# A planned one-core graph/convolution/GRU kernel on Trainium2: residual loaded a batch ahead, tanh and mix chained by expected times, third weight added behind its load, VectorE given background work further ahead

## The chip, the cores and the metric

The kernel runs on one core of one Trainium2 chip. The metric is the device time of one execution in microseconds. Before the change it is 2330.36 us, the median of three runs (2320.62 to 2338.33).

## What is computed

The input `x` is 32 batches of 512 nodes with 256 channels; `adj` is a 0/1 matrix of 512 x 512 for each batch. All is float32. Cut to what matters (`d` = 256):

```python
h  = relu(layernorm(x))
xc = transpose(h)                                          # channels first
c  = bn2(conv1d_17taps(relu(bn1(conv1d_1tap(xc)))))
x_conv = transpose(relu(c + xc))
s   = h @ w_se.T + b_se                                    # 3 numbers per node
A   = exp(-dist(s, s)) * adj
msg = relu(h @ w_msg.T + b_msg)
x_nmp = einsum('bnm,bmd->bnd', A, msg)
gi = concat([x_conv, x_nmp]) @ w_ih.T + b_ih
gh = h @ w_hh.T + b_hh
r, z = sigmoid(gi_r + gh_r), sigmoid(gi_z + gh_z)
n  = tanh(gi_n + r * gh_n)
out = x + (1 - z) * n + z * h
```

## The kernel before, in words

**Tiles and stages.** Channels lie on the 128 partitions (two halves, `ND` = 2), nodes along the free dimension; P is 128. Each batch goes through six streams, each a Python generator that issues instructions and then says when it can go on:

- `begins` and `rows` (`begin`, `norm_t`, `conv1`; L320, L770, L785): the normalised input is turned by TensorE, stored to DRAM (`hd`), and the 1-tap convolution writes into `h1`. The layer norm's statistics are background work of VectorE (`norm`, L273).
- `graphs` (`graph`, L794): `messages` (tiles `msg`, `aug`), `factors` and `factors_t` (`augl`, `augr` turned into `left`, `right`), `kernel_exp` (four matmuls and Exp into `at`), `masked` (four times a mask times `at`), `gather` (`at` times `msg`, copied into `right` and stored to DRAM as `nd`).
- `conv` (`convolution`, L610): the 17 taps by a two-level product scheme: batches in groups of four, eight groups of 25 products. Product m needs the operand `X2[m]` (tiles `x`, VectorE), the weight `WS[m]` (tile `w`) and, from group 1 on, `XD[m]` (tile `xd`, VectorE). Results go through PSUM tiles `ps_c` and `ps_b` and are summed by VectorE into `n`, `z` and `y` (`summed`, L485). In group 0 the weights are made by VectorE and ScalarE (`weights_first`, L425) and stored; in group 1 two thirds of each weight are loaded and the last third is added by VectorE (`third_weight`, L473); later groups load all three.
- `gates` (`gates`, L824): `evacuate` (L555) copies `y` into `xconv`; then the products with `whh` and `wih` in PSUM tiles `ps_acc`, sigmoid, tanh (`mix`, L889) and three VectorE operations into `o_sb` (`mix_last`, L858).
- `finish` (L753): TensorE turns `o_sb`, VectorE adds the original input (tile `res`, loaded by `load_res`, L763), SyncE stores it.

**What sets the order.** Nothing reorders at run time: each engine and each engine's DMA queue goes through its list in order, and waits on semaphores. The lists are made by a planner in the kernel itself (L936 to L1049). It keeps a clock `now` of TensorE's planned work and, for VectorE and ScalarE, the planned time `free` at which each is done. In each step it picks, among streams whose awaited time has come, the one with the smallest `clock` and lets it issue up to its next `yield`. If none is able, `now` moves on by 0.25. After each step `fill` (L964) issues what was put off with `later`, tries one `evacuate`, and gives VectorE background work (operands, sums, statistics, weights) while `dve.free < now + 0.5`. A `yield act.free + 0.2` thus says: go on 0.2 us after ScalarE's planned end. The planner knows of no DMA queue, of no PSUM bank that must be emptied before its next use, and of no activation table load.

**Loads around the change.** Nearly all loads and the output stores are issued on SyncE's queue. `load_res(b)` is called by `mix_last` of batch b, ahead of the loads of the next batch's sums (`load_sums`, tiles `xnb`), and the finish of batch b comes at least 6 planned us later. The two `res` tiles of a batch fill the pool's two buffers. `w` has three buffers; its loads wait for the product that last read the buffer. PSUM: three banks for `ps_g` (shared by turning, messages, exp, gather and 1-tap convolution), two for `ps_acc`, two for `ps_c`, one for `ps_b`.

Of the kernel before, what the change touches and what calls it, by code (L numbers as in the profile page):

```python
# [44 lines left out]
def kernel(  # L45
# [50 lines left out]


    now = 10.0

    def elements(t):  # L100
        n = 1
# [40 lines left out]

    def later(t, f):
        LATER.append((t, f))

    def settle():
        while LATER:
# [125 lines left out]
    def norm(b):  # L273

        xs = XS[b]
        st = front.tile([P, NT, 6], F32, name="st")
        mv = front.tile([P, NT, 2], F32, name="mv")
        for c in range(NT):
            dve.bn_stats(st[:, c, :], xs[:, c, :])
            dve.bn_aggr(mv[:, c, :], st[:, c, :])  # L280
            if c % 2:
                yield 0.0
        rstd = front.tile([P, NT], F32, name="rstd")
        rsqrt(rstd, mv[:, :, 1])
        yield dve.free + 1.5
        shift = front.tile([P, NT], F32, name="shift")
        dve.scalar_tensor_tensor(
            shift, mv[:, :, 0], -1.0, rstd, op0=ALU.mult, op1=ALU.mult
        )
        yield dve.free + 0.2  # L290
        for c in range(NT):
            act.activation(
                xs[:, c, :], xs[:, c, :], AF.Identity, bias=shift[:, c : c + 1],
                scale=rstd[:, c : c + 1],
            )
            if c % 2:
                yield act.free + 0.2

    def norm_some(b):

# [124 lines left out]
    def weights_first():  # L425


        outer = [
            taps_of(
                lambda k, i=i: wraw[:, i, :, :, k, :],  # L430
                lambda i=i: prep.tile([P, 2, 3, D], F32, name=f"g{i}", bufs=1),
                True,
            )
            for i in range(ND)
        ]
        for j1 in ORDER:
# [12 lines left out]
            for j2 in ORDER:  # L449
                gg = []  # L450
                for i in range(ND):
                    gg.append(next(inner[i]))
                    yield 0.0
                yield dve.free + 0.1
                w = new_w()
                for i in range(ND):
                    act.activation(
                        w[:, :2, i, :], gg[i], AF.Copy, scale=GSCALE[j1] * GSCALE[j2]
                    )
                nc.scalar.dma_start(WD[len(WS)][:, :2], w[:, :2])  # L460
                WS.append(w)
                W_AT.append(act.free + 0.2)
                yield 0.0

    def weights_again(m):
# [19 lines left out]
    def summed(g):  # L485
# [29 lines left out]
        for j1 in ORDER:  # L515
# [30 lines left out]
                for f in range(3):  # L546
                    add(y[:, :, f], y[:, :, f], z, ALU.subtract if (f, j1) == (1, 2) else ALU.add)
        SUMS.append(lambda: EVAC.extend(
            (y, b, o) for b in range(g * G, (g + 1) * G) for o in range(ND)
        ))  # L550
        yield

# [1 line left out]

    def evacuate():  # L555

        y, b, o = EVAC[0]
        if b >= G and b - G not in gated or act.free > now + 0.3:
            return False
        EVAC.pop(0)  # L560
        act.behind(dve)
        if o == 0:
            XC[b] = late.tile([P, ND, Q * U], F32, name="xconv", bufs=4)
        c = o * NU + b % G * U
        act.activation(
            XC[b][:, o, :].rearrange("p (u h k) -> p k h u", h=2, k=9),
            y.rearrange("p e f (h n) -> p (e f) h n", h=2)[:, :, :, c : c + U],
            AF.Identity, bias=bn2_sh[:, o : o + 1], scale=bn2_sc[:, o : o + 1],
        )
        if o == ND - 1:  # L570
            evacuated[b] = act.free + 0.2
        return True

    AHEAD = 3
# [11 lines left out]
    def operand_some():  # L586

        nonlocal freed
        if len(X2) >= min(at_product + 1 + AHEAD, 25 * NG) or len(X2) >= 25 * made:
            return False  # L590
        if len(X2) == 25 * (made - 1) and now < made_at:
            return False
        got = next(xs)
        if got is not None:
            X2.append(got)
            X_AT.append(dve.free + 0.2)
            if len(X2) % 25 == 21:
                freed = len(X2) // 25
        return True
# [10 lines left out]
    def convolution():  # L610
# [18 lines left out]
        for g in range(NG):  # L629
# [3 lines left out]
            for n in range(25):  # L633
# [5 lines left out]
                if m == 24:  # L639
                    late_pools()  # L640
                yield lambda: len(X2) > m and len(WS) > m
                if 25 <= m + 1 < 50:
                    third_weight(m + 1)
                for k in (m, m + 1):
                    if 25 <= k < len(X2) and k not in XD:
                        XD[k] = ends(X2[k])
                        X_AT[k] = dve.free + 0.2
# [40 lines left out]
    def messages(b, msg, c):  # L688
# [3 lines left out]
        dve.tensor_tensor(gr.aug[:, c, :3], ps[:, D:], bmsg[:, D:], op=ALU.add)  # L692
        if c % 2:
            m = msg[:, c - 1 : c + 1, :]
            later(dve.free + 0.1, lambda: act.activation(m, m, AF.Relu))

    def factors():
        aug, augl = gr.aug, gr.augl
# [48 lines left out]
    def gather(b, msg, at, d):  # L747
        ps = bank()
        matmul_sum(ps, [(msg[:, c, d * P : (d + 1) * P], at[:, c, :]) for c in range(NT)])
        act.activation(gr.right, ps, AF.Copy)  # L750
        nc.scalar.dma_start(ND_[b, d], gr.right)

    def finish(b, o_sb, c):  # L753
        ps = bank()
# [6 lines left out]
        nc.sync.dma_start(out[b].rearrange("(c p) d -> p c d", p=P)[:, c : c + 2, :], y)  # L761

    def load_res(b):  # L763
        for c in range(0, NT, 2):
            XR[b, c] = late.tile([P, 2, D], F32, name="res", bufs=2)
            nc.sync.dma_start(XR[b, c], x[b].rearrange("(c p) d -> p c d", p=P)[:, c : c + 2, :])

# [17 lines left out]
    def rows(b):  # L785
        nonlocal made, made_at
        for o in range(ND):
            conv1(b, o)
            if o == ND - 1 and b % G == G - 1:
                made, made_at = b // G + 1, act.free + 0.2  # L790
            yield now
        HT.pop(b, None)

    def graph(b):  # L794
# [18 lines left out]
        yield act.free + 0.2  # L813
        for n in range(NT):
            masked(b, at, n)
            if n < NT - 1:
                yield dve.free - 0.4
        settle()
        yield dve.free + 0.2
        for d in range(ND):  # L820
            gather(b, msg, at, d)
            yield now
# [1 line left out]
    def gates(b):  # L824
# [26 lines left out]
        def residual():  # L851
            xconv = XC.pop(b)[:, :, :N]
            dve.tensor_tensor(xconv, xconv, hT, op=ALU.add)
            yield dve.free + 0.1
            act.activation(xconv, xconv, AF.Relu)
            x_in.extend([xconv[:, i, :] for i in range(ND)] + [XN[b, d] for d in range(ND)])

        def mix_last(r, z, o):  # L858
            t = o_sb[:, o, :]
# [2 lines left out]
            dve.tensor_tensor(t, r, t, op=ALU.add)  # L862
            if o == ND - 1:
                unfinished[b] = o_sb
                load_res(b)
                load_sums(b + 1, 0)
                load_sums(b + 1, 1)

        for o in range(ND):
            r = z = None  # L870
# [17 lines left out]

            def mix():  # L889
                dve.tensor_tensor(r, ps_n, r, op=ALU.add)  # L890
                later(dve.free + 0.1, lambda r=r, o=o: act.activation(
                    r, r, AF.Tanh,
                    bias=vec[:, _COL["b_ih"] + 2 * ND + o : _COL["b_ih"] + 2 * ND + o + 1],
                ))
                later(dve.free + 1.0, lambda r=r, z=z, o=o: mix_last(r, z, o))

            ps_r = acc.tile([P, N], F32, name="ps_acc")
            if o == 0:
# [4 lines left out]
                yield act.free + 0.2  # L903
# [15 lines left out]
    def all_finishes():  # L919
        for b in range(B):  # L920
            yield lambda: b in unfinished
            yield max(dve.free, now + 6.0)
            for c in range(0, NT, 2):
                finish(b, unfinished[b], c)
                yield now


    bn1_sc, bn1_sh = bn_affine("bn1")
# [13 lines left out]
        return True  # L942

    def norm_ahead(early=0.45):
        for b in list(NORMS):
# [37 lines left out]
    def all_rows():  # L983
        nonlocal rows_wait
        for b in range(B):
            if b < G:
                yield from begin(b)
                yield act.free + 0.2
# [7 lines left out]

    def all_gates():
        yield lambda: late is not None
        for b in range(B):
            yield from gates(b)  # L1000

# [97 lines left out]
```

## Time and profile before

| what | us |
|---|---|
| median of three runs | 2330.36 |
| the profiled execution's own time | 2333.51 |
| its span, first to last instruction | 2331.6 |
| TensorE busy | 2186.6 (94%) |
| VectorE busy | 1453.7 (62%) |
| ScalarE busy | 783.0 (34%) |
| mean granted TensorE clock | 0.975 |

In the rows of the profile PE is TensorE, DVE VectorE, ACT ScalarE, SP SyncE; "SPq" is SyncE's DMA queue issuing a transfer. A row of a group or of the timeline names the line, the engine, the operation, the tile written and the tiles read, the shape, and the count; in square brackets, or behind the second bar, stands the idle time of the engine just before and what ended it. A float32 matmul of the program stands as two in the trace. Nearly every row has L126, L131 or L117, since helpers issue for all streams; so one goes by the tiles' names. In a row of the windows view stand, for each engine, its busy time and number of instructions, then the granted TensorE clock and the share of the DMA engines in use.

### The profile page before, as it was taken

The page shows a single profiled execution, that of the slowest core. Times are in us where ns is not written, and L with a number is a line of the kernel's source. Part 1 is how long each engine was busy: PE and PEld are TensorE (multiplying, and loading weights), DVE is VectorE, ACT ScalarE, POOL GpSimd, SP SyncE. Part 2 cuts the span into 40 slices and gives each one's busy share as a digit, 9 for nine tenths or more (in the row PEclk, how much of TensorE's full clock was granted, in tenths as well). Part 3 has the DMA queues.
Part 4 walks back from the last instruction along what each step waited for, and adds up shares of the span by engine and source line. Part 5 has one row for each costly group of instructions (what it writes and reads, how often), then busy time and mean ns, then how long its engine had stood idle before and what let it go on. Part 6 is the DMA issues. An engine that isn't in the chain of part 4 may idle for free.

```text
span 2331.6 us, 26175 instructions
## 1 busy us (share of the span) xinstructions
PE 2186.6 (94%) x9640; PEld 1359.6 (58%) x9640; DVE 1453.7 (62%) x2700; ACT 783.0 (34%) x1318; POOL 60.6 (3%) x73
## 2 busy tenths in 40 slices
PE   5888989999989999999989998999999999999998
PEld 3765655566556656566556565655656656566443
DVE  6566667767666666766556665666766846576422
ACT  5342432134322333234412334223432334222411
POOL 1000000000000000000000000000000000000000
PEclk9998989999999999999999999999999999999999
DMA  6343454455544545554355534556545535444121
GB/s 248 125 148 117 178 181 149 136 199 149 167 140 140 185 127 163 151 160 152 127 162 157 176 114 131 166 158 176 163 134 155 158 132 158 153 136 136 50 73 45
DMA packets 328270, 342.40 MB, mean 147 GB/s; under 512 B 214160, under 2 KB 263696, under 8 KB 327504
## 3 DMA queue, kind: packets, MB, share of 16 engines
q1 hardware_dynamic: 308720, 287.52, 40.6%
q10 hardware_dynamic: 17424, 46.67, 5.2%
q0 software_dynamic: 2000, 6.56, 0.7%
q8 instruction: 76, 1.25, 0.2%
q14 instruction: 50, 0.41, 0.1%
HBM read 270.68 MB, written 69.99 MB: 146 GB/s over the span
## 4 chain that ended last, share of the span: by engine, by line
PE 83%; DVE 6%; ACT 5%; DMA 4%; issue 1%; SPq 0%; ACTq 0%; DVEq 0%
PE ps_acc L126 40%; PE ps_g L126 17%; PE ps_c L126 16%; PE ps_b L126 6%; PE ps_g L131 3%; DMA nd<-right 1%; PE ps_b L724 1%; DMA res<-in_x_dram 1%; DVE o_sb L117 1%; ACT at L117 1%; ACT r L117 1%; DMA w<-wd 1%; DMA xnb<-nd 1%; DVE x L117 1%; ACT L117 1%
## 5 line engine op out<-in xcount | busy, mean ns | idle before, releaser
L126 PE MATMUL ps_acc<-hTb,whh 128*128 128x512 f32 x768 | 366.3, 607 | 13.3 <-ACT r L117 13.3
L126 PE MATMUL ps_c<-xd,w 128*128 128x116 f32 x2800 | 349.6, 279 | 21.1 <-DVE xd L117 12.2
L126 PE MATMUL ps_acc<-xconv,wih 128*128 128x512 f32 x768 | 363.9, 596 | 4.6 <-ACT xconv L117 4.6
L126 PE MATMUL ps_acc<-xnb,wih 128*128 128x512 f32 x768 | 362.7, 594 | 2.8 <-DMA xnb<-nd 2.6
L126 PEld LDWEIGHTS ps_c<-xd,w 128*128 128x128 f32 x2800 | 334.2, 195 | 25.3 <-DVE xd L117 13.1
L126 PE MATMUL ps_g<-at,msg 128*128 128x512 f32 x512 | 233.5, 604 | 11.8 <-DVE at L117 10.2
L126 PEld LDWEIGHTS ps_acc<-hTb,whh 128*128 128x128 f32 x768 | 142.9, 194 | 169.8 <-issue 141.9
L126 PEld LDWEIGHTS ps_acc<-xnb,wih 128*128 128x128 f32 x768 | 141.5, 189 | 165.1 <-issue 158.2
L126 PEld LDWEIGHTS ps_acc<-xconv,wih 128*128 128x128 f32 x768 | 141.8, 191 | 160.3 <-issue 149.7
L126 PEld LDWEIGHTS ps_b<-x,w 128*128 128x128 f32 x1400 | 182.8, 193 | 77.1 <-issue 58.0
L117 DVE TENSOR_TENSOR r<-ps_acc,r 128x512 f32<-128x512 f32 x64 | 44.2, 691 | 267.0 <-PE ps_acc L126 267.0
L126 PE MATMUL ps_b<-x,w 128*128 128x116 f32 x1400 | 185.6, 276 | 7.2 <-ACT at L117 7.0
L117 ACT ACTIVATE mid<-ps_b 128x232 f32<-128x232 f32 x175 | 63.6, 363 | 339.2 <-PE ps_b L126 322.3
L126 PEld LDWEIGHTS ps_g<-at,msg 128*128 128x128 f32 x512 | 96.9, 194 | 126.5 <-issue 109.5
L117 DVE SCALAR_TENSOR_TENSOR r<-ps_acc,vec,r 128x512 f32<-128x512 f32 x64 | 48.0, 751 | 184.1 <-PE ps_acc L126 149.5
L126 PE MATMUL ps_g<-wmsg,hTg 128*128 128x259 f32 x512 | 131.9, 395 | 23.2 <-DVE aug L117 13.2
L117 DVE SCALAR_TENSOR_TENSOR x<-x,x 128x480 f32<-128x480 f32 (+1 forms) x184 | 143.8, 782 | 2.0
L117 ACT ACTIVATE right<-ps_g 128x512 f32<-128x512 f32 x96 | 57.3, 597 | 257.7 <-PE ps_g L126 227.5
L117 ACT ACTIVATE z<-ps_acc,brz 128x512 f32<-128x512 f32 x64 | 43.9, 686 | 276.0 <-PE ps_acc L126 275.9
L117 DVE TENSOR_TENSOR x<-x 128x240 f32<-128x240 f32 (+1 forms) x320 | 135.6, 462 | 0.3
L126 PEld LDWEIGHTS ps_g<-wmsg,hTg 128*128 128x128 f32 x512 | 97.3, 196 | 61.6 <-issue 35.3
L126 PE MATMUL ps_g<-hT,w 128*128 128x512 f32 x256 | 123.9, 630 | 3.9 <-ACT hT L117 2.7
(101 smaller groups left out, 2463.5 us busy)
## 6 DMA issues: line engine op xcount, KB each, us to landing
w<-wd SPq DMA_DIRECT2D x150, 768.0 KB, 4.6
m_sb<-in_adj_dram SPq DMA_DIRECT2D x384, 64.0 KB, 2.6
hd<-hT ACTq DMA_DIRECT2D x32, 512.0 KB, 5.0
hTg<-hd SPq DMA_DIRECT2D x32, 512.0 KB, 3.6
nd<-right ACTq DMA_DIRECT2D x64, 256.0 KB, 2.1
hTb<-hd SPq DMA_DIRECT2D x32, 512.0 KB, 5.2
xnb<-nd SPq DMA_DIRECT2D x64, 256.0 KB, 3.1
res<-in_x_dram SPq DMA_DIRECT2D x64, 256.0 KB, 4.0
```

The lines of the kernel that those rows point to most:

```text
L117: getattr(self.engine, name)(*tiles, **more)
L126: nc.tensor.matmul(ps, lhsT, rhs, **more)
L131: nc.tensor.transpose(ps, a, ident)
L724: nc.tensor.matmul(pss[c], gr.left[k, :], gr.right[k, :], start=True, stop=True, tile_position=(32 * c, 0),)
```

## The change

1. `load_res(b + 1)` is called behind the finish of batch b (and `load_res(0)` when the gates start). The finish of b no longer waits for `now + 6`, but for `dve.free + 0.6`. `load_sums` of the next batch is issued by the last `mix`, not by `mix_last`.
2. `later` keeps its list sorted by time. `mix` puts off only the tanh; the tanh (`mix_next`) then puts off `mix_last` to 0.3 behind its planned end.
3. `third_weight` is added a product ahead only if the weight's load is planned to have landed, else at its own product; the product then waits for the planned end of the addition.
4. `fill` gives VectorE background work while `dve.free < now + 1.5`, where it was 0.5.
5. Most waits for VectorE or ScalarE have one margin, `LAG` = 0.6, where they had 0.1 to 0.3. `evacuate` waits until the planned end of the sums has passed. Of the statistics only the first two batches in line are tried. The second gather of a batch uses a part of `at` in place of `right`. The gates' clock starts at 1.25 instead of 1.2.

The diff, cut to its core:

```diff
 def later(t, f):
     LATER.append((t, f))
+    LATER.sort(key=lambda e: e[0])
...
+thirds = set()
 def third_weight(m):
+    if m in thirds:
+        return
+    thirds.add(m)
     w = WS[m]
     dve.tensor_tensor(w[:, 2], w[:, 0], w[:, 1], op=ALU.add)
     nc.gpsimd.dma_start(WD[m % 25][:, 2], w[:, 2])
+    W_AT[m] = dve.free + LAG
...
 def evacuate():
-    y, b, o = EVAC[0]
-    if b >= G and b - G not in gated or act.free > now + 0.3:
+    t, y, b, o = EVAC[0]
+    if now < t or b >= G and b - G not in gated or act.free > now + 0.3:
         return False
     EVAC.pop(0)
-    act.behind(dve)
...
     # convolution, before product m
-    if 25 <= m + 1 < 50:
+    if 25 <= m + 1 < 50 and W_AT[m + 1] <= now:
         third_weight(m + 1)
...
     yield max(X_AT[m], W_AT[m])
+    if 25 <= m < 50:
+        third_weight(m)
+        yield W_AT[m]
...
 def gather(b, msg, at, d):
...
-    act.activation(gr.right, ps, AF.Copy)
-    nc.scalar.dma_start(ND_[b, d], gr.right)
+    sums = gr.right if d == 0 else at[:, 0, :]
+    act.activation(sums, ps, AF.Copy)
+    nc.scalar.dma_start(ND_[b, d], sums)
...
     # graph
     factors()
     load_graph(b + 1)
-    yield dve.free + 0.2
+    yield dve.free + LAG
     factors_t()
...
-    yield act.free + 0.3
+    yield act.free + LAG
     kernel_exp(at)
-    yield act.free + 0.2
+    yield act.free + 0.3
...
+def mix_next(r, z, o):
+    act.activation(r, r, AF.Tanh, bias=...)
+    later(act.free + 0.3, lambda: mix_last(r, z, o))
 def mix_last(r, z, o):
...
     if o == ND - 1:
         unfinished[b] = o_sb
-        load_res(b)
-        load_sums(b + 1, 0)
-        load_sums(b + 1, 1)
 def mix():
     dve.tensor_tensor(r, ps_n, r, op=ALU.add)
-    later(dve.free + 0.1, lambda r=r, o=o: act.activation(r, r, AF.Tanh, bias=...))
-    later(dve.free + 1.0, lambda r=r, z=z, o=o: mix_last(r, z, o))
+    later(dve.free + 0.3, lambda r=r, z=z, o=o: mix_next(r, z, o))
+    if o == ND - 1:
+        load_sums(b + 1, 0)
+        load_sums(b + 1, 1)
...
 def all_finishes():
     for b in range(B):
         yield lambda: b in unfinished
-        yield max(dve.free, now + 6.0)
+        yield dve.free + LAG
         for c in range(0, NT, 2):
             finish(b, unfinished[b], c)
             yield now
+        load_res(b + 1)
...
 def fill():
...
-    while dve.free < now + 0.5 and background():
+    while dve.free < now + 1.5 and background():
...
-    "gates": (all_gates(), 125.0, 1.2),
+    "gates": (all_gates(), 125.0, 1.25),
```

Since these numbers feed the planner, the lists of all engines change. Three places follow, as the lists stand before and with the change.

SyncE's queue around the end of the gates of batch 9 of 32 (`res` is the residual, `xnb` the sums of the next batch, `w` a convolution weight, `hT` and `hTb` stored inputs). Before:

```order
L264 DMA m_sb<-in_adj_dram 32x16x32 x12
L766 DMA res<-in_x_dram 128x2x256 x2
L185 DMA xnb<-nd_0_132 128x512
L185 DMA xnb<-nd_1_133 128x512
L469 DMA w<-wd_230 128x1536
L761 DMA out_dram<-res 128x2x256 x2
L469 DMA w<-wd_231 128x1536
```

With the change:

```order
L187 DMA xnb<-nd_0_132 128x512
L187 DMA xnb<-nd_1_133 128x512
L171 DMA hT<-hd_98 128x1024
L471 DMA w<-wd_232 128x1536
L772 DMA out_dram<-res 128x2x256 x2
L777 DMA res<-in_x_dram 128x2x256 x2
L171 DMA hT<-hd_99 128x1024
```

The load of `res` stood two loads and a weight ahead of the store that ends the same batch; now it stands right behind that store and is for the next batch.

TensorE in group 0 of the convolution, at the third graph before and the second with the change (`wmsg` products are the messages, `augl` and `augr` are turned into the factors, `left` gives the exp, `m_sb` are masks, `ps_c` convolution products). Before:

```order
L126 MATMUL ps_c<-x_885,w 128x116 x16
L126 MATMUL ps_g<-wmsg,hTg 128x259 x8
L131 MATMUL ps_g<-ident,augl 128x128
L131 MATMUL ps_g<-ident,augr 128x128 x4
L724 MATMUL ps_b<-right,left 128x512
L724 MATMUL ps_g<-right,left 128x512 x3
L131 MATMUL ps_g<-ident,m_sb 128x128 x4
```

With the change:

```order
L127 MATMUL ps_g<-wmsg,hTg 128x259 x6
L127 MATMUL ps_c<-x_830,w 128x116 x16
L127 MATMUL ps_g<-wmsg,hTg 128x259 x2
L127 MATMUL ps_c<-x_818,w 128x116 x16
L132 MATMUL ps_g<-ident,x_sb 128x128 x4
L132 MATMUL ps_g<-ident,augl 128x128
L132 MATMUL ps_g<-ident,augr 128x128 x4
L734 MATMUL ps_b<-right,left 128x512
L734 MATMUL ps_g<-right,left 128x512 x3
```

The turning of `augl`, which needs VectorE's work on the last message, followed that message's matmul at once; now a convolution product and a turning stand between.

VectorE in the first products of group 1 (`w<-w` is the addition of a third weight, `xd` the operand of a product, `y` the sums of a group). Before:

```order
L117 TENSOR_TENSOR n<-ps_c,mid 128x464
L117 TENSOR_TENSOR x_2217<-x_2064 128x240 x2
L117 TENSOR_TENSOR w<-w 128x512
L117 SCALAR_TENSOR_TENSOR z<-n 128x464
L117 TENSOR_TENSOR y<-y,z 128x3x464 x3
L117 TENSOR_TENSOR z<-ps_c,mid 128x464
L117 TENSOR_TENSOR msg<-ps_g,bmsg 128x256
L117 TENSOR_TENSOR aug<-ps_g,bmsg 128x3
```

With the change:

```order
L118 SCALAR_TENSOR_TENSOR z<-n 128x464
L118 TENSOR_TENSOR at<-ps_g,at 128x4x128
L118 TENSOR_TENSOR y<-y,z 128x3x464
L118 TENSOR_TENSOR w<-w 128x512
L118 TENSOR_TENSOR xd<-x_1868 128x480
L118 TENSOR_TENSOR w<-w 128x512
L118 TENSOR_TENSOR at<-ps_g,at 128x4x128
L118 TENSOR_TENSOR y<-y,z 128x3x464
```

The additions now stand beside the `xd` of the products that need them, with the three long `y` additions spread among other work instead of in one row behind an addition.

More of the change, by code (lines that the diff above doesn't have):

```diff
@@ L98 @@
     now = 10.0
+    LAG = 0.6
     def elements(t):
@@ L548, in summed @@
         SUMS.append(lambda: EVAC.extend(
-            (y, b, o) for b in range(g * G, (g + 1) * G) for o in range(ND)
+            (dve.free + 0.3, y, b, o) for b in range(g * G, (g + 1) * G) for o in range(ND)
         ))
@@ L694, in messages @@
             m = msg[:, c - 1 : c + 1, :]
-            later(dve.free + 0.1, lambda: act.activation(m, m, AF.Relu))
+            later(dve.free + 0.3, lambda: act.activation(m, m, AF.Relu))
     def factors():
@@ L763, in load_res @@
     def load_res(b):
-        for c in range(0, NT, 2):
+        for c in range(0, NT if b < B else 0, 2):
             XR[b, c] = late.tile([P, 2, D], F32, name="res", bufs=2)
@@ L853, in residual @@
             dve.tensor_tensor(xconv, xconv, hT, op=ALU.add)
-            yield dve.free + 0.1
+            yield dve.free + 0.3
             act.activation(xconv, xconv, AF.Relu)
             x_in.extend([xconv[:, i, :] for i in range(ND)] + [XN[b, d] for d in range(ND)])
+        def mix_next(r, z, o):
+            act.activation(
+                r, r, AF.Tanh,
+                bias=vec[:, _COL["b_ih"] + 2 * ND + o : _COL["b_ih"] + 2 * ND + o + 1],
+            )
+            later(act.free + 0.3, lambda: mix_last(r, z, o))
         def mix_last(r, z, o):
@@ L890, in mix @@
                 dve.tensor_tensor(r, ps_n, r, op=ALU.add)
[L891 to L894, printed above, removed]
-                later(dve.free + 1.0, lambda r=r, z=z, o=o: mix_last(r, z, o))
+                later(dve.free + 0.3, lambda r=r, z=z, o=o: mix_next(r, z, o))
+                if o == ND - 1:
+                    load_sums(b + 1, 0)
+                    load_sums(b + 1, 1)
             ps_r = acc.tile([P, N], F32, name="ps_acc")
@@ L944, in norm_ahead @@
     def norm_ahead(early=0.45):
-        for b in list(NORMS):
+        for b in list(NORMS)[:2]:
             if (b < G or clock["conv"] >= (b - G) / G - early) and norm_some(b):
```

21 lines of the change are left out of this document (11 added, 10 removed).

## The prediction

> **What bounds the kernel now.** I read the page first, then who waited for whom, then the timeline just before each long wait of TensorE, then the clock around those waits.
>
> ```profile
> span 2331.6 us, 26175 instructions
> PE 2186.6 (94%) x9640; PEld 1359.6 (58%) x9640; DVE 1453.7 (62%) x2700; ACT 783.0 (34%) x1318; POOL 60.6 (3%) x73
> ```
>
> TensorE sets the end: it idles 2331.6 - 2186.6 = 145 us in the whole span, and the change removes none of its matmuls. So a gain can only come out of those 145 us and out of time at a reduced clock. TensorE's waits by the engine that ended them, and VectorE's own long ones (us in total, times, longest):
>
> ```profile
> PE ps_acc L126 <- ACT r L117: 13.3, 11, 5.1
> PE ps_g L126 <- DVE aug L117: 13.2, 4, 9.3
> PE ps_c L126 <- DVE xd L117: 12.2, 5, 6.5
> PE ps_g L126 <- DVE at L117: 10.2, 5, 3.8
> PE ps_g L131 <- DVE augr L117: 10.1, 7, 2.4
> PE ps_c L126 <- DVE z L117: 8.9, 3, 4.5
> PE ps_g L126 <- DVE res L117: 8.6, 2, 5.9
> ...
> DVE res L117 <- DMA res<-in_x_dram: 48.4, 14, 7.2
> ...
> DVE z L117 <- ACT y L117: 21.4, 7, 3.9
> ...
> DVE w L117 <- DMA w<-wd: 15.5, 6, 6.1
> ```
>
> Six of these rows end on VectorE: 13.2 + 12.2 + 10.2 + 10.1 + 8.9 + 8.6 = 63.2 us in 26 waits. VectorE is busy only 62%, so it is not short of time; it is late, because its list goes in order and at times it stands waiting for a transfer: 48.4 us for `res`, 15.5 us for `w`. What such a wait does:
>
> ```profile
> 692.74 0.39 SPq L766 DMA_DIRECT2D res<-in_x_dram  x1
> ...
> 695.63 0.69 DVE L117 TENSOR_TENSOR res<-ps_g,res 128x512 f32<-128x512 f32 x1 [2.75 <-DMA res<-in_x_dram]
> 696.24 0.65 DVE L117 TENSOR_TENSOR xd<-x 128x480 f32<-128x480 f32 x1
> ...
> 696.94 1.42 PE L126 MATMUL ps_c<-xd,w 128*128 128x116 f32 x5 [6.45 <-DVE xd L117]
> ```
>
> The load is issued at 692.74; VectorE stands at the addition that needs it; `xd` queues behind; TensorE idles 6.45 us for `xd`. The row that names `xd` hides a late load.
>
> **The change part by part.** (a) *Residual a batch ahead.* The same chain ends at four other places, and a fifth comes through VectorE's backlog:
>
> ```profile
> 857.90 1.12 PE L126 MATMUL ps_acc<-xnb,wih 128*128 128x512 f32 x2 [2.18 <-DMA xnb<-nd]
> 977.74 1.58 PE L126 MATMUL ps_c<-xd,w 128*128 128x116 f32 x11 [2.86 <-DVE xd L117]
> 1194.29 2.09 PE L126 MATMUL ps_g<-wmsg,hTg 128*128 128x259 f32 x4 [5.94 <-DVE res L117]
> 1415.98 1.51 DVE L117 TENSOR_TENSOR res<-ps_g,res 128x512 f32<-128x512 f32 x2 [6.43 <-DMA res<-in_x_dram]
> 1422.79 1.22 PE L126 MATMUL ps_acc<-hTb,whh 128*128 128x512 f32 x1 [2.40 <-ACT r L117]
> 1747.41 2.10 PE L126 MATMUL ps_g<-wmsg,hTg 128*128 128x259 f32 x4 [2.62 <-DVE res L117]
> ```
>
> The load now has a whole batch, some 60 us, to land, so all of it goes: 6.45 + 2.18 + 2.86 + 5.94 + 2.40 + 2.62 = 22 us (bounds 17, if the 2.86 and the 2.62 have another cause just behind, and 22). The price is on SyncE's queue: the load of `res` stands behind the store of the same buffer and waits until that has landed.
>
> ```profile
> out_dram<-res SPq DMA_DIRECT2D x64, 256.0 KB, 2.6
> ```
>
> 2.6 us in each of 32 batches, with a `w` or a stored input queued behind it. A weight is loaded into a third buffer, two products ahead, which hides it: I take 0. With that cover gone it would be 32 x 2.6 = 83 us.
>
> (b) *Third weight.*
>
> ```profile
> 303.84 0.32 SPq L469 DMA_DIRECT2D w<-wd  x1
> ...
> 305.18 0.69 DVE L117 TENSOR_TENSOR w<-w 128x512 f32<-128x512 f32 x1 [6.13 <-DMA w<-wd]
> ...
> 306.45 4.64 DVE L117 TENSOR_TENSOR y<-y,z 128x1392 f32<-128x1392 f32 x3
> ...
> 312.42 1.20 PE L126 MATMUL ps_g<-wmsg,hTg 128*128 128x259 f32 x2 [9.27 <-DVE aug L117]
> ```
>
> VectorE waits 6.13 us for a weight loaded late, three `y` additions of 4.64 us follow in one row, and the messages come last. With the condition and the new order both causes go: 9 us. Bound below 4, if SyncE's queue is late again and only the `y` row is spread.
>
> (c) *Tanh and mix chained.* One place shows its cost:
>
> ```profile
> 624.75 0.60 ACT L117 ACTIVATE right<-ps_g 128x512 f32<-128x512 f32 x1 [4.55 <-DMA m_sb<-in_adj_dram]
> 625.75 0.72 ACT L117 ACTIVATE r<-r,vec 128x512 f32<-128x512 f32 x1 [0.40 <-ACT right L117]
> ...
> 630.33 1.58 PE L126 MATMUL ps_g<-wmsg,hTg 128*128 128x259 f32 x4 [2.99 <-DVE aug L117]
> ```
>
> The second copy into `right` waits for the first one's store, the tanh stands behind it, `o_sb` on VectorE behind the tanh, the messages behind `o_sb`. The second tile for the gather and the chain undo it: 3 us (0 to 3).
>
> (d) *Wider margins and more background work.* The lists show where it acts. Costing rows of the order at TensorE's rate between matmuls,
>
> ```profile
> 280.47 7.13 PE ps_c L126 x64
> ...
> 761.97 6.88 PE ps_g L126 x16
> ```
>
> 7.13 / 64 = 0.111 us for a narrow one and 6.88 / 16 = 0.43 us for a wide one (two of each per matmul of the program), six of the first seven graphs had nothing between the last message and the turning of `augl`; now one has nothing and the others 2.7 to 8.7 us. Between exp and gather stood 5.3 to 12.4 us in the first five graphs; now it is 16 or more in four of them. These are the waits for `augr` (10.1) and `at` (10.2); I take 13 of their 20. Bounds 0 and 20: group 0 could be held by VectorE itself (a rival below).
>
> The same edit lets VectorE be 1.0 us further ahead with background work, so what TensorE waits for stands up to 1.0 us later in its queue. The planner allows for that where it has a margin, but not where a PSUM bank must be emptied. Bounds 0 and 26 (26 waits x 1.0). Against the high end: of 189 banks of `ps_g` that VectorE empties after messages and finishes, 53 had under 2.7 us of TensorE work before their next use, now 15. I take 13 as what comes back here and as new waits elsewhere.
>
> (e) *Clock.* The granted clock after each long wait (third number from the right):
>
> ```profile
> 696.90:702.50 5.60, 5.56 (x19) 4.53 (x20) 4.62 (x9) 0.00 (x0) 0.00 (x0) 0.50 0.31 90
> 859.50:863.00 3.50, 3.50 (x13) 2.49 (x13) 3.04 (x8) 0.91 (x3) 0.00 (x0) 0.51 1.01 339
> 1194.00:1198.00 4.00, 3.71 (x9) 2.90 (x10) 3.54 (x9) 1.67 (x2) 0.00 (x0) 0.57 0.86 260
> 1747.00:1750.50 3.50, 3.09 (x7) 2.50 (x8) 3.50 (x7) 0.10 (x1) 0.00 (x0) 0.51 0.77 231
> 312.40:320.00 7.60, 6.23 (x22) 4.98 (x23) 6.04 (x18) 5.08 (x9) 0.54 (x1) 0.50 0.28 103
> 1953.00:1957.00 4.00, 4.00 (x27) 3.00 (x26) 3.97 (x6) 3.57 (x6) 0.00 (x0) 1.00 0.18 70
> ```
>
> Half a clock costs half the stretch: 2.8 + 1.7 + 1.7 + 1.7 + 3.8 = 12 us behind waits that go. I take 12 (bounds 8 and 25, if the small waits' dips go too). The last row shows that a wait of 2.4 us need not cost any. The Trainium skill, "TensorE: Matmul & The Clock Gate", section "What's actually happening", lets the clock fall only after an idle window of about 3.4 us. By it the dips behind the 2.18 and 2.62 us waits would not be there and the term would be 8 (2.8 + 1.7 + 3.8), the forecast 4 us longer; the trace disagrees at 859.5 and 1747.0 (0.51) and agrees at 1953.0.
>
> (f) *ScalarE* gets four more activation table loads (56 for 52 in the lists).
>
> ```profile
> L117 ACT ACT_TABLE_LOAD x52 | 66.7, 1283 | 27.5 <-issue 11.8 <-PE ps_acc L126 9.6 <-DMA x_sb<-in_x_dram 4.6
> ```
>
> 4 x 1.283 = 5 us on an engine busy 34%; hidden by its idle time except before a sigmoid, so 1 (0 to 5). The other edits (later clock of the gates, statistics of two batches, planned `evacuate`) move work that TensorE does anyway: 0.
>
> Sum: 22 + 9 + 3 + 13 + 12 = 59 us gained, 13 + 1 = 14 given back, 45 net. The profiled execution took 2333.5 us, 3.1 above the median of the runs; so 2288.5 for it, and 2285 for the median.
>
> **The rivals.** *All of VectorE's lateness goes.* The 63 us in six rows, 3 us for the tanh's copy and 25 us of clock: about 90 us, 2240. For it: VectorE's idle share. Against it: VectorE also waits 21.4 us for ScalarE's copies of `y` before it can write `z`, and the change leaves those.
>
> *Group 0 is held by VectorE.* From its first product to the first of group 1:
>
> ```profile
> 54.40:292.20 237.80, 208.24 (x1221) 158.92 (x1221) 145.87 (x286) 95.11 (x180) 6.80 (x6) 0.92 0.40 143
> ```
>
> By the lists the TensorE work in this stretch falls from 184 to 148 us (three gathers are done in it, not six), while VectorE's 145.9 us of work stays. If the stretch still lasts 238 us, 36 us of TensorE work come on top later, and the 13 of (d) are lost: 59 - 13 - 14 - 36 = -4, so 2334, no change. For it: VectorE is busy only 61% here with work that is needed. Against it: 92 us of its idle time lie here, and being allowed 1.5 ahead is what fills them.
>
> *Slower: banks held by VectorE.* If each of the 189 banks it empties after messages and finishes is freed 0.5 us later with no TensorE work in between, that is 95 us; less the net of 45, 50 us slower: 2380. It decides from (45 / 189) 0.24 us a bank on. For it: the planner knows no banks. Against it: the counts under (d).
>
> *The edit does not do what it says*: SyncE's queue, unknown to the planner, stays late, and the third weight and `xnb` wait as before. That costs 9 + 2 of the gain and their clock, 5: 2301, inside the forecast.
>
> **How the numbers follow.** The forecast with its unknowns (2265 to 2306) has 0.60; VectorE's lateness gone (2225 to 2265) 0.16; group 0 held, about no change, 0.17; banks, slower, 0.07. About 1%, 23 us, is what a measurement of this kernel tells from no change. Faster by more (below 2307) is the first two, 0.76; the same 0.17; slower 0.07. The range takes in the forecast, the nearer three quarters of the second case and the third up to its own figure, and leaves out the slower one: 2240 to 2334, some 0.8.
>
> **What would show it.** Right: VectorE's wait for `res` near zero, its wait for `w` under 5 us, the waits for `aug`, `xd`, `augr` and `at` at half or less, and TensorE idle near 105 us with a granted clock of 0.98 or more. Group 0 held: the stretch to group 1's first product stays near 238 us, with waits on `x` or `w`. Banks: new waits of `ps_g` on `msg` or `res` additions. It would be wrong if TensorE's idle time stayed near 145 us with other names in its rows.

## The result, and the profile after

The changed kernel takes 2239.48 us (median of four runs, 2237.55 to 2241.54) beside 2334.27 us for the kernel before in the same comparison: a ratio of 0.9604, 95% interval 0.9561 to 0.9647. By the ratio that is about 92 us, twice the 45 us forecast. The median lies half a microsecond below 2240, which is both the lower edge of the range and the number of the rival in which all of VectorE's lateness goes; the forecast itself, 2285, is missed by 45 us. The profiled execution took 2241.54 us.

The same first lines of the page, of the changed kernel:

```profile
span 2239.7 us, 26162 instructions
## 1 busy us (share of the span) xinstructions
PE 2154.9 (96%) x9640; PEld 1346.7 (60%) x9640; DVE 1450.3 (65%) x2700; ACT 787.7 (35%) x1322; POOL 56.7 (3%) x73
```

TensorE's idle time fell from 145.0 to 84.8 us (2239.7 - 2154.9), and its busy time by 31.7 us with the same 9640 matmuls. A busy matmul can be one at half clock or one that overlaps badly, so idle time alone tells two thirds of the gain. The mean granted clock rose from 0.975 to 0.989.

TensorE's waits in the changed kernel, by the engine that ended them, and two of VectorE's (us in total, times, longest):

```profile
PE ps_g L127 <- ACT hT L118: 11.4, 2, 10.4
PE ps_g L127 <- DMA hT<-hd: 8.8, 2, 4.6
PE ps_acc L127 <- ACT xconv L118: 5.2, 4, 1.3
PE ps_b L127 <- DVE w L118: 5.1, 3, 3.2
...
PE ps_g L127 <- DVE at L118: 3.7, 3, 1.4
...
PE ps_acc L127 <- ACT r L118: 2.7, 5, 1.4
...
PE ps_g L132 <- DVE augr L118: 1.6, 2, 1.3
...
PE ps_g L127 <- DVE res L118: 1.1, 3, 0.4
...
DVE o_sb L118 <- ACT r L118: 17.9, 11, 4.2
...
DVE w L118 <- DMA w<-wd: 0.4, 1, 0.4
```

Of the six rows that made 63.2 us before, `aug`, `xd` and `z` have no row left and the other three make 3.7 + 1.6 + 1.1 = 6.4 us. VectorE's row for the residual is gone (48.4 before), its wait for `w` is 0.4 (15.5), its wait for the tanh 17.9 (69.3 over 38 times by the same view of before). New or longer are waits for `hT` (3.2 before) and its load (none) and for `w` (0.2): 11.4 + 8.8 + 5.1 = 25 us stand there now, 10.4 of them at the start of the program.

The stretch from the first convolution product to the first of group 1, and what follows (us, then busy time and instructions of TensorE, its weight loads, VectorE, ScalarE and GpSimd, then clock and DMA):

```profile
69.20:239.30 170.10, 158.57 (x1069) 133.38 (x1068) 135.73 (x258) 80.72 (x152) 5.34 (x5) 0.96 0.45 163
239.30:2239.70 2000.40, 1961.64 (x8466) 1193.86 (x8464) 1282.72 (x2345) 670.81 (x1097) 41.10 (x46) 0.99 0.48 150
```

It took 237.8 us before and takes 170.1; VectorE is busy 80% of it (135.73 of 170.10) where it was 61%.

To compare many kernels I use one more number, worked out from the records: for every matmul, the time by which the next one starts later than the first one's own rate (0.429, 0.217, 0.111 and 0.109 us for 512, 259, 116 and 128 columns; matmuls that run side by side count for nothing). The sum is the time that TensorE loses after its first matmul, to waits and to half clock alike. Before it is about 210 us: 88 in the first 400 us of the span, 122 later. In the changed kernel it is 116: 60 and 56. So 28 us of the gain lie early and 66 in the steady part, where the forecast had put 22 + 3 us of waits and their clock. By the same count TensorE loses 52 us in the stretch above before and 22 with the change, so about 30 of its 68 us are a gain; the rest is work that now comes later, since three gathers lie in it where six did. Ahead of the stretch the loss grows from 18 to 29 us: the first product starts at 69.2 us instead of 54.2, behind the long wait for `hT`.

### The profile page after: what moved, and what is told of

Its sections match the earlier page's. It is cut to its first block, busy times and chain, and to the rows that moved or that the text cites. A ratio compares the mean times of both kernels' runs of the same rounds, so it can differ in the third digit from the quotient of the medians.

```text
span 2239.7 us, 26162 instructions
## 1 busy us (share of the span) xinstructions
PE 2154.9 (96%) x9640; PEld 1346.7 (60%) x9640; DVE 1450.3 (65%) x2700; ACT 787.7 (35%) x1322; POOL 56.7 (3%) x73
## 3 DMA queue, kind: packets, MB, share of 16 engines
q8 instruction: 76, 1.25, 0.2%
## 5 line engine op out<-in xcount | busy, mean ns | idle before, releaser
L127 PE MATMUL ps_acc<-hTb,whh 128*128 128x512 f32 x768 | 357.7, 594 | 2.8 <-ACT r L118 2.7
L127 PE MATMUL ps_c<-xd,w 128*128 128x116 f32 x2800 | 342.1, 275 | 0.0
L127 PEld LDWEIGHTS ps_c<-xd,w 128*128 128x128 f32 x2800 | 328.4, 192 | 5.1 <-issue 4.8
L127 PE MATMUL ps_g<-hT,w 128*128 128x512 f32 x256 | 122.5, 622 | 22.1 <-ACT hT L118 11.4
L118 ACT ACTIVATE h<-ps_g,bn_shift,bn_scale 128x252 f32<-128x252 f32 (+1 forms) x192 | 81.0, 495 | 119.2 <-PE ps_g L127 118.0
L118 DVE TENSOR_TENSOR msg<-ps_g,bmsg 128x256 f32<-128x256 f32 x128 | 53.5, 419 | 103.6 <-PE ps_g L127 103.2
```

What stands on the lines that cost most here:

```text
L118: getattr(self.engine, name)(*tiles, **more)
L127: nc.tensor.matmul(ps, lhsT, rhs, **more)
```

## The experiments

Theory L, the prediction's: VectorE is late because its list stands waiting for transfers, and the gain is the residual, the third weight and the tanh's chain. Theory S: the spacing (margins, and background work further ahead) carries most of it. Theory O, formed on the way: the parts remove the same waits, so none of them can be told by its size alone.

| kernel | median us | ratio to before, 95% interval | lost in the first 400 us, later | first product of group 1 at |
|---|---|---|---|---|
| before | 2330 to 2334 | 1 | 88, 122 | 292 |
| changed | 2239.5 | 0.9604 [0.9561, 0.9647] | 60, 56 | 239 |
| b_res | 2305.1 | 0.9881 [0.9864, 0.9897] | 92, 91 | 292 |
| b_far | 2272.1 | 0.9739 [0.9721, 0.9757] | 58, 89 | 235 |
| b_lag | 2322.8 | 0.9961 [0.9947, 0.9975] | 108, 89 | 316 |
| b_gates (1.25) | 2279.2 | 0.9773 [0.9755, 0.9792] | 87, 68 | 289 |
| b_g130 | 2324.0 | 0.9973 [0.9958, 0.9987] | 85, 110 | 288 |
| b_g115 | 2373.1 | 1.0181 [1.0138, 1.0223] | 81, 165 | 288 |
| a_g120 | 2259.9 | 0.9690 [0.9669, 0.9711] | 58, 79 | 237 |
| a_g130 | 2259.2 | 0.9680 [0.9659, 0.9702] | 62, 68 | 239 |
| a_near | 2264.8 | 0.9717 [0.9692, 0.9743] | 92, 48 | 292 |
| a_res_late | 2236.7 | 0.9588 [0.9567, 0.9608] | 59, 53 | 238 |
| a_lag02 | 2241.2 | 0.9603 [0.9578, 0.9628] | 65, 53 | 238 |
| a_third_old | 2241.6 | 0.9608 [0.9588, 0.9628] | 67, 51 | 237 |

Kernels named b_ are the one before with one part of the change; those named a_ are the changed one with one part taken back. They are compared by their ratios; 0.001 is 2.3 us.

**One part alone.**

b_res:

```diff
         if o == ND - 1:
             unfinished[b] = o_sb
-            load_res(b)
...
             for c in range(0, NT, 2):
                 finish(b, unfinished[b], c)
                 yield now
+            load_res(b + 1)
```

> The kernel before with the residual loaded a batch ahead and nothing else. Theory L (VectorE is late because its list stands waiting for transfers): the 48.4 us of waiting for the residual go, with them the 22 us of TensorE's waits behind it and about 7 us at half clock: 26 to 34 us faster. Theory S (most of the gain comes from spacing, that is from wider margins and from VectorE working further ahead): 10 to 20 us faster, since other late work takes over behind the same matmuls.

It gains 28 us (ratio 0.9881): within theory L's 26 to 34, though the medians alone, 25 us apart, lie just short of it. The waits of TensorE and VectorE in it:

```profile
PE ps_g L126 <- DVE aug L117: 14.5, 4, 10.6
PE ps_c L126 <- DVE z L117: 11.9, 3, 4.5
PE ps_acc L126 <- ACT r L117: 10.9, 10, 5.1
PE ps_g L131 <- DVE augr L117: 10.1, 7, 2.4
PE ps_g L126 <- DVE at L117: 9.8, 5, 3.5
...
PE ps_c L126 <- DVE xd L117: 2.9, 3, 1.3
...
PE ps_g L126 <- DVE res L117: 0.3, 1, 0.3
...
DVE o_sb L117 <- ACT r L117: 69.6, 38, 4.9
...
DVE w L117 <- DMA w<-wd: 17.4, 5, 7.4
```

VectorE's wait for the residual's load has no row left (48.4 before), and with it TensorE's waits for `xd` (12.2 before) and `res` (8.6) are nearly gone; the other rows stand much as before. The cost of that wait was read rightly from the chains `res`, `xd`, `ps_c`. The planner knows of no DMA queue, so this edit changes SyncE's queue alone: in the two traces TensorE, VectorE, ScalarE and GpSimd go through the same instructions in the same order (9640, 2700, 1318 and 73). The 28 us are thus the residual's, and no luck of a new list.

b_far:

```diff
-    while dve.free < now + 0.5 and background():
+    while dve.free < now + 1.5 and background():
...
-    for b in list(NORMS):
+    for b in list(NORMS)[:2]:
```

> The kernel before with VectorE given background work while it is less than 1.5 us ahead instead of 0.5, and with the statistics of two batches only, which this needs; nothing else. Theory S: TensorE's waits for xd, z, augr and at shrink and it is 30 to 50 us faster, though VectorE still waits about 48 us for the residual. Theory L: within 10 us of before, since VectorE still stands at the same transfers. Theory B (banks held longer by VectorE): slower, with new waits of ps_g on the additions of msg.

The ratio of 0.9739 is 61 us: more than theory S asked for, far outside theory L's 10, and nothing of theory B.

```profile
PE ps_g L126 <- DMA hT<-hd: 15.6, 2, 8.2
...
PE ps_g L126 <- DVE aug L117: 3.7, 2, 3.0
...
PE ps_g L131 <- DVE augr L117: 2.6, 2, 1.3
...
DVE res L117 <- DMA res<-in_x_dram: 35.7, 9, 8.7
...
DVE w L117 <- DMA w<-wd: 11.8, 4, 4.7
```

And group 0's stretch in it:

```profile
67.00:234.80 167.80, 160.03 (x1062) 132.66 (x1061) 133.50 (x252) 79.29 (x152) 6.18 (x6) 0.96 0.49 170
```

VectorE still waits 35.7 us for the residual and 11.8 for `w`, and yet `aug` and `augr` are nearly gone, and TensorE's rows for `xd` and `z` are gone wholly: an engine that has its work in the queue earlier can stand waiting without making TensorE wait. Group 0's stretch falls from 237.8 to 167.8 us with VectorE busy 80% of it, and TensorE loses 19 us in it beside 52. So theory L falls as the main cause. Of the loss, about 30 us go in the first 400 us and 33 later. The early part is no luck of the list: in all seven kernels with 1.5 group 1 begins at 235 to 239 us, in all seven with 0.5 at 288 to 316. The later part can be, as the next runs show.

b_lag (the margin 0.6 at the places that had 0.2 or 0.3, as in the change's diff, but for the third weight and the finish):

```diff
-                yield act.free + 0.2
+                yield act.free + LAG
...
-        yield dve.free + 0.2
+        yield dve.free + LAG
         factors_t()
```

> The kernel before with the margin 0.6 wherever the change has it outside the third weight and the finish, and nothing else. Theory S: 15 to 30 us faster, the waits for augr, at and for the sigmoid of r shrink. Theory L: within 10 us of before.

9 us: within theory L's 10, and the margin is not where theory S has its gain. The early loss even grows (108 beside 88): the first convolution product starts at 75.0 us instead of 54.2, and TensorE loses 36 us ahead of it beside 18.

b_gates, meant to show how much a new list by itself can do:

```diff
-    "gates": (all_gates(), 125.0, 1.2),
+    "gates": (all_gates(), 125.0, 1.25),
```

> The kernel before with the starting value of the gates' clock at 1.25 instead of 1.2 and nothing else: all lists are drawn up anew with no cause of waiting removed. Both theories: within 15 us of before either way; how far it moves says how much of any other single edit can be the luck of a new list.

Both theories were wrong: one starting value, with no cause of waiting removed, gains 53 us. What ended VectorE's idle time before the addition of the residual in it, and three of TensorE's waits:

```profile
its engine sat idle before it (us, times) until:
  PE ps_g L131: 12.3, 11
```

```profile
PE ps_g L126 <- DVE aug L117: 16.0, 6, 6.2
...
PE ps_g L126 <- DVE at L117: 10.8, 5, 3.8
PE ps_g L131 <- DVE augr L117: 10.3, 8, 1.3
```

VectorE no longer waits for the residual at all, although its load is issued at the same place of the program. Worked out from the issue of each batch's first `res` load and the end of its last `o_sb`: before, the load is issued after `o_sb` is done in 8 of 32 batches (by up to 5.3 us), since SyncE's queue stands at something else; here it is 3.1 us or more ahead in all 32. The early waits (`aug`, `at`, `augr`) stay, and so does the early loss.

b_g130, and b_g115 with 1.15 in the same place:

```diff
-    "gates": (all_gates(), 125.0, 1.2),
+    "gates": (all_gates(), 125.0, 1.3),
```

> The kernel before with the starting value of the gates' clock at 1.3 (before 1.2; 1.25 alone gave 2279 us beside 2331). Theory M (a later start of the gates is better in itself): 2265 to 2285 us, again no wait of VectorE for the residual. Theory P (1.25 was a lucky phase of loads against products): anywhere from 2275 to 2335, with the wait for the residual back in some batches.

> The kernel before with the starting value of the gates' clock at 1.15 (before 1.2). Theory M: at or above before, 2330 to 2370 us. Theory P: anywhere from 2275 to 2335 us; below 2310 speaks against M.

2324 and 2373 us: not monotone, so theory M falls; and 1.15 lies above what theory P allowed, so the scatter is wider than I thought: 94 us between the best and the worst of four values. Rows that have grown in them, of 1.3 and then of 1.15:

```profile
PE ps_g L131 <- DVE augr L117: 17.0, 16, 2.2
...
PE ps_g L131 <- ACT left L117: 12.0, 6, 5.1
```

```profile
PE ps_g L126 <- DMA hT<-hd: 16.2, 6, 5.3
PE ps_acc L126 <- ACT xconv L117: 14.7, 9, 2.6
...
DVE res L117 <- DMA res<-in_x_dram: 47.7, 21, 6.1
```

With 1.3 VectorE does not wait for the residual either, and still 110 us are lost in the steady part. TensorE's waits for the factors grow by some 12 us (`augr` 10.1 and `left` 6.5 before); the rest of that loss is spread over many rows, and no run tells its cause. With 1.15 VectorE waits for the residual in 21 places, and TensorE waits for `hT` loads (no row before) and for the xconv of the gates (4.6 before). So the phase between the gates and the convolution sets which chain is tight.

**One part taken back.**

a_g120, and a_g130 with 1.3 in the same place:

```diff
-    "gates": (all_gates(), 125.0, 1.25),
+    "gates": (all_gates(), 125.0, 1.2),
```

> The changed kernel with the gates' clock starting at 1.2 as before, all else as changed. If the 51 us that 1.25 gave alone come on top of the other parts, 2270 to 2290 us. If they are the same waits that the residual, the chain and the background work remove (theory O, overlap), within 12 us of the changed kernel, 2230 to 2250 us.

> The changed kernel with the gates' clock starting at 1.3 instead of 1.25, all else as changed. In the kernel before the values 1.15, 1.2, 1.25 and 1.3 gave 2373, 2331, 2279 and 2324 us. If the change has made the program less open to the phase of gates against convolution (theory R): 2235 to 2265 us, as 1.2 gave 2260. If 1.25 is a lucky phase in both: 2265 to 2300 us.

20 and 18 us slower than with 1.25. For 1.2 that lies between the two expectations: part of the phase's gain is the same as that of the other parts, part comes on top. It speaks for theory R as far as three values go: over 1.2, 1.25 and 1.3 the kernel before spreads over 52 us (2279 to 2331), the changed one over 20 (2239.5 to 2260); 1.15, the worst value before, was not tried with the change. How much of the 92 us is phase depends on the order of counting. With the start moved first, it is worth 53 us and the rest of the change 40 (2279.2 to 2239.5); with the rest first, that is worth 71 at 1.2 (65 at 1.3) and the start 20 on top. Counted the first way, the table shows where the 40 lie: 87 to 60 early, in group 0, and 68 to 56 later.

a_near:

```diff
-    while dve.free < now + 1.5 and background():
+    while dve.free < now + 0.5 and background():
```

> The changed kernel with VectorE's background work at most 0.5 us ahead as before (1.5 in the change), all else as changed. Theory S (spacing carries much of the gain): 2265 to 2290 us, with waits for augr, at, z and xd back. Theory L (waiting for transfers was the cause, and the change has removed it): within 12 us of the changed kernel.

26 us slower (0.9717 - 0.9604 is 0.0113), at the lower edge of theory S. The loss is all early, as group 0's stretch and one wait show:

```profile
69.00:291.90 222.90, 198.86 (x1187) 156.21 (x1187) 144.23 (x285) 91.31 (x170) 4.76 (x5) 0.92 0.40 140
```

```profile
PE ps_g L132 <- DVE augr L118: 7.0, 6, 1.3
```

Group 0's stretch lasts 222.9 us, beside 170.1 with the change and 237.8 before, and group 1 begins at 292 us as it did before. TensorE loses 48 us in the stretch beside 22, which is the whole 26; `augr` is back, but the steady part loses 48 us, less than the 56 of the changed kernel. So in company with the other parts the background work further ahead is needed only while VectorE makes weights, operands and sums at once.

a_res_late:

```diff
         if o == ND - 1:
             unfinished[b] = o_sb
+            load_res(b)
...
-            load_res(b + 1)
```

> The changed kernel with the residual loaded by the last mix of its own batch again, all else as changed (the finish still comes 0.6 us behind the mix, so the load has less time than it had before). Theory L: VectorE waits for it in nearly all 32 batches, 60 us or more of its time, TensorE loses 25 to 60 us: 2265 to 2300 us. Theory O (other parts hide the same waits): within 12 us of the changed kernel.

2236.7 us, no slower than the changed kernel (0.9588 beside 0.9604, intervals that overlap). What the addition of the residual waited for:

```profile
its engine sat idle before it (us, times) until:
  PE ps_g L132: 11.8, 11
  DMA res<-in_x_dram: 2.5, 3
```

Theory L expected 60 us here and gets 2.5: with the rest of the change the load is issued 3.2 us or more ahead of the end of `o_sb` in all 32 batches, as it is in b_gates, and nearly always lands in time. The four engines' lists are the same as in the changed kernel here too, so this is no luck of a list. The edit that the change names first is worth 28 us by itself and nothing in company. That holds for the gates' start at 1.25, which takes the residual's wait away by itself (b_gates); with the start at 1.2 it was not tried.

a_lag02:

```diff
-    LAG = 0.6
+    LAG = 0.2
```

> The changed kernel with the common margin at 0.2 instead of 0.6, all else as changed. Theory S: 10 to 25 us slower than the changed kernel, with small waits of TensorE behind ScalarE and VectorE back. Luck of the list alone: within 20 us either way with no one wait grown.

2241.2 us, no difference: the margin is not needed.

a_third_old:

```diff
-    if 25 <= m + 1 < 50 and W_AT[m + 1] <= now:
+    if 25 <= m + 1 < 50:
         third_weight(m + 1)
...
     yield max(X_AT[m], W_AT[m])
-    if 25 <= m < 50:
-        third_weight(m)
-        yield W_AT[m]
...
-    W_AT[m] = dve.free + LAG
```

> The changed kernel with the third weight added a product ahead whether or not its load is due, as before; all else as changed. The prediction's term: VectorE's wait for w back at about 15 us, all of it in group 1, and 9 us plus 4 us at half clock lost, near 2252 us. If the background work 1.5 us ahead hides it: within 5 us of the changed kernel.

2241.6 us: hidden. One long wait of a weight's addition is left; the view puts it down to a mask's load, though the weight's own load lands in the same moment. Some 12 us behind it TensorE waits once for a `z`:

```profile
PE ps_c L127 <- DVE z L118: 5.1, 1, 5.1
...
DVE w L118 <- DMA m_sb<-in_adj_dram: 4.8, 1, 4.8
```

That `z` stands behind three `y` additions in one row, as in the kernel before, so it can't be put down to the weight alone. The loads of the weights are no longer late enough to matter, with the condition or without.

Not tried: the chain of tanh and mix with the second tile of the gather, alone or taken back. VectorE's wait for the tanh differs much among kernels that have the chain (17.9 us at 1.25, and by the same view 40.0 at 1.2 and 26.7 at 1.3) and among those that have not (69.3 before, 24.8 in b_gates). Whether the chain or the earlier finish is what holds the changed kernel's steady loss between 56 and 79 us at all three starting values, where before it is 68 to 122, stays open.

## Why the prediction was half right

**What bounds it** was right: TensorE sets the end, VectorE was late and not short of time, and the gain came out of TensorE's 145 us and the half clock. The signs that it named came too: VectorE's wait for `res` gone, for `w` 0.4 us, the waits for `aug`, `xd`, `augr` and `at` under half, a clock of 0.989, and idle time at 85 us where 105 was forecast. But with the residual's edit taken back they come too (a_res_late: 2.5 us for `res`, 0.2 for `w`, idle time 82 us), so they could not tell which part did it.

**(a) The residual**, 22 us and some clock, measured 28 alone, with all engines' lists unchanged: right as a size for the kernel before, and no luck. That it would be the residual's edit that brings it in the change is not so: without it the changed kernel is as fast. The store that the load now stands behind costs SyncE's queue 46.0 us in all by the view of its waits, in 62 waits of at most 1.3; a_res_late, which has no such order, is no faster beyond the noise: 0 was right.

**(b) The third weight**, 9 us: the wait went (15.5 to 0.4 us), but the condition was not needed for it (a_third_old). The reading of the example was off: the load at 303.84 is the next weight's. The one that VectorE waited for until 305.18 was issued long before and was slow to land, as the critical chain of before shows (start, us):

```profile
295.16 9.93 DMA w<-wd
```

**(c) The chain**, 3 us, was not tried by itself; no run shows its size.

**(d) Margins and background work** is the step that failed. I booked 13 us gained in group 0 and 13 given back, because work that TensorE waits for stands up to 1.0 us later behind more background work. Run alone, the background work further ahead gained 61 us, some 30 of them surely its own, and gave back nothing that shows on the `msg` additions. So the two sides of the term stood the wrong way round. The spacing that I read from the lists and credited to the margins comes in good part from the background work. Costed as in the prediction, the work between exp and gather in the first five graphs is 5.3 to 12.4 us before and again in b_lag, and 10.2 to 20.4 in b_far. Of the first seven graphs, six turn `augl` right behind the last message before, three in b_lag, two in b_far, five with the change but 0.5 (a_near), one with the change. The planner counts VectorE's work in hand as time to wait for, so with more of it the streams that need VectorE go on later and TensorE gets other work in between. In group 0's stretch TensorE loses 52 us before, 55 with the margins alone, 19 with the background work alone. The mistake was to price only the delay in the queue. Work handed over earlier is also done earlier, and what TensorE waits for here (`x`, `xd`, the sums that free `ps_c`) is itself such background work; and VectorE's waits for transfers then fall into time that it has in hand. How much each of these brings was not measured. The margins gain 9 us alone and nothing in company.

**The later clock of the gates** I booked at 0, as work that is done anyway. It gains 53 us alone and 20 in company. This step failed by its reason too: in lists that are fixed ahead, a start moved by 0.05 of a group moves every later load and product against each other.

**(e) The clock**, 12 us, was too small. By the mean granted clock, half speed cost (1 - 0.975) x 2331.6 = 58 us before and (1 - 0.989) x 2239.7 = 25 us with the change, 33 less, some of it in time that was idle anyway. Counting only what the matmuls that start at half clock lose, each at most its own rate, it is 41 us before and 20 with the change: 21 less, inside the bounds of 8 and 25. Behind a wait of 4.59 us for an `hT` load the clock is at half for most of the next 3.6 us; behind one of 1.4 us for `r` in the gates it stays full:

```profile
929.40:933.00 3.60, 3.60 (x5) 1.59 (x6) 0.00 (x0) 0.21 (x1) 0.00 (x0) 0.60 0.71 243
```

```profile
1320.60:1324.00 3.40, 3.40 (x19) 2.44 (x20) 3.37 (x6) 2.63 (x3) 0.00 (x0) 1.00 0.91 169
```

By the idle window of about 3.4 us that the Trainium skill gives ("TensorE: Matmul & The Clock Gate", section "What's actually happening") both should be so; the trace of before, with its dips behind 2.18 and 2.62 us, still says that less can do.

**(f) The table loads** (56) cost little that shows: all TensorE's waits for `r` in the gates are 2.7 us. No run tells the four more apart.

**The sum.** By itself each part looks like a good share: 28 + 61 + 9 + 53 = 151 us for four of them, where the whole is 92. They remove the same waits. The other way round, taking one back costs 26 and 20 us and three times nothing. So neither the sum of parts alone nor the sum of parts taken back is the gain. A sum of waits read from one trace held for the part that leaves the engines' lists as they are (22 and some clock, 28 measured). It failed where an edit draws up the lists anew: 13 less 13 against 61 in (d), 0 against 53 for the gates' start.

**The rivals.** VectorE's lateness gone, 2240 us: this is what came, with the six rows at 6.4 us; my objection, the copies of `y`, did not hold, since that wait has no row in the changed kernel. That the number fits is luck in part: 20 us of it are the gates' start, which the rival left out (2260 without it), and some 22 us went to waits that are new or grew, which it did not count. Group 0 held by VectorE: it fell, with 170 us for the stretch and VectorE busy 80%. About the stretch it comes nearer in a_near, where 0.5 keeps it at 223 us. Banks held by VectorE: no sign. SyncE's queue stays late: not for the weights and `xnb` that it named (0.4 us and no row), but in small for `hT` loads. This one is issued 6.4 us ahead of the product that needs it, where half of these loads take 5.1 us or more to land:

```profile
922.93 0.33 SPq L171 DMA_DIRECT2D hT<-hd  x1
...
929.37 1.19 PE L127 MATMUL ps_g<-hT,w 128*128 128x512 f32 x1 [4.59 <-DMA hT<-hd]
```

## What to carry to other kernels

Where lists are fixed ahead and an engine is late though not busy, first hand it its work earlier, and only then look after single waits: here one constant took some 30 us out of the first stage, which no other edit did, and the residual's load, worth 28 us alone, was worth nothing beside the other edits. Before crediting an edit that redraws all lists, redraw them by an edit that means nothing (a start moved a little, either way): the scatter of that (94 us here) is the yardstick for every single experiment, unless the engines' lists stay the same, as they did with the residual's edit: such a run can be read to its noise. And test a part both alone and by taking it back, since parts that remove the same wait look large in the one and like nothing in the other.

## What I had not expected of the hardware

Nothing in the engines or their rates was new. What surprised was how far one queue's order reaches: the same load instruction at the same place of the program kept VectorE waiting 48.4 us in all at one starting value of the gates and not at all at another.
